# A two-layer graph network with routed experts: the experts' second product as seven block products

## The chip, the cores and the metric

The kernel runs on one core of one Trainium2 chip. A core has five engines with in-order queues of their own: TensorE (PE: matmuls, with the loads of their weights shown apart as PEld), VectorE (DVE), ScalarE (ACT), GpSimd (POOL) and SyncE (SP, which issues most transfers); data lies in SBUF (128 partitions) and products appear in PSUM banks. The metric is the device time of the core in microseconds. A profile is one execution of its own; its time is given beside the median of the runs without a profile.

## The reference

A graph of N = 3327 nodes with D = 256 features goes through two layers. Each adds an aggregation over the dense adjacency matrix `adj`, and then a mixture of eight experts, of which every node uses two:

```
# layer 0
x = x + relu(adj @ (layernorm(x) @ W) + b)
t = layernorm(x)
e1, e2 = top_2(t @ Wg.T + bg);  p1, p2 = softmax of the two scores
x = x + sum over e in (e1, e2):  p_e * (relu(t @ W1[e].T + b1[e]) @ W2[e].T + b2[e])     # hidden 1024
# layer 1
f = tanh(adj * adj), kept where adj > 0 (the 700 largest of a row)
h = tanh(layernorm(x) @ W_proj + b_proj)
x = x + relu(f @ (h @ W_gcn) + b_gcn)
x = x + t + sum over two experts of p_e * (gelu(t @ w1[e] + b1[e]) @ w2[e] + b2[e])      # t = layernorm(x), hidden 256
```

All of it is float32. The change concerns the product with `W2[e]` in layer 0 and the bias and the weight behind it.

## The kernel before

The nodes are padded to 3328, 26 tiles of 128. `x` stays in SBUF; six large buffers of SBUF, the `ring`, hold whatever streams in (pieces of the adjacency matrix, weights of experts, rows), and one more, `pad`, holds the small operands of a block of tokens.

**Layer 0, aggregation** (`aggregate_first`, L482). Thirteen panels of 256 nodes. Pairs of panels are made from seven half-size products in place of eight (`pair`, with sums made by VectorE in place). The last panel is done alone. For each finished pair, `weigh` (L504) multiplies the sums by W and writes to `x`, `route` computes the row norms and the gate scores and picks two experts for each node, and `list_tokens` (L756, through `list_waiting` and `listed`) counts places with two tiny matmuls a tile (L767, L768), turns the scores into weights (the exponential, L759) and scatters each node's normalised row, with its weight (column WT) and its target row (ID), by GpSimd's indirect DMA into a DRAM list sorted by expert (`scatter`, L788). What is left for the last panel, `finish` (L512), is handed to the experts and runs inside their first block. There it first lists the tokens of the last pair (`listed()`), then weighs the last panel's two tiles, then routes that panel.

**Layer 0, experts** (`experts`, L1060). The lists are worked off in blocks of up to SB = 256 tokens of one expert, two groups of 128 each (SG = 2). There are 30 blocks: 26 pair blocks with two groups and 4 with one ("singles"). The first EARLY = 8 blocks are pairs known early; the later order is one single after every four pairs. `step` (L1242) does a block t:

- it issues the loads of block t + 2 on SP's queue (rows xb, W1, b1, W2, b2; each block takes two of the six ring buffers, so three blocks are in flight);
- `first` (L1175): for each of eight chunks of 128 hidden features, two matmuls of 128 weight columns by 256 tokens into a PSUM bank (L1182; two banks, `psh`), then bias and ReLU by ScalarE into `hT` (L1189);
- on block 0 alone, `between` = `finish`;
- `turned` (L1165): TensorE transposes the rows of block t + 1 (L1168), and `copy`, VectorE's tensor_copy in layer 0, brings them to SBUF (L1172);
- `second` (L1192): VectorE makes the target rows (L1202, L1203). For each group eight matmuls with 128 tokens of `hT` as weights and 256 columns of W2 moving are summed in a PSUM bank (L1220; four banks, `psy`); VectorE adds b2 (L1227), multiplies by the token's weight (L1228), and GpSimd scatters the rows into the DRAM array `ys0` (L790).

```
for hc in range(hc_n):
    last_product[:] = [nc.tensor.matmul(ps, lhsT=hT[:, hc, ts(g, P)], rhs=w2[:, hc, :], ...)]
nc.vector.tensor_tensor(y[:, g, :], ps, bb2, ALU.add)
last_y[:] = [nc.vector.tensor_scalar(y[:, g, :], y[:, g, :], xb[:, g, WT : WT + 1], None, ALU.mult)]
```

Matmuls in float32 are two records each in the trace.

**The order on the engines.** Each engine works its queue strictly in order. The order in a queue comes from the framework's scheduler, which works with estimated costs; `tc.issue_after(...)` and the kernel's `behind(...)` (L293) put an instruction behind a given one. `last_y` and `last_product` are the latest instruction of their kinds, for that use.

**Around and after the experts.** After block 1 `load_gate(gates[1])` (L1430) broadcasts the second layer's gate matrix from DRAM to `gate`, an SBUF tile of 128 x 2048, through GpSimd's queue (1 MB); `gate` held the first layer's gate before, for VectorE's products in `scores` (L659). The next use is layer 1's routing. Behind block 27, `add_begun` (L1473) adds outputs of tiles done by then to `x` (six additions, L1304), and behind block 28 `statistics` of 12 tiles (from L337) starts their layernorm. When all 30 blocks are done, `between` (L1521) issues what leads to layer 1: the rest of the outputs is loaded on SP's queue behind the scatters of `ys0`, added, normalised (L371), transposed (L387) and multiplied by the two matrices; the first pieces of the transposed adjacency are loaded and filtered. Then follow layer 1's aggregation (`aggregate`, L430), its experts and the output.

Of the kernel before, what the change touches and what calls it, by code (L numbers as in the profile page):

```python
# [10 lines left out]
F32 = mybir.dt.float32  # L11
# [11 lines left out]
P = 128  # L23
# [104 lines left out]
def gnn_moe_two_layers(  # L128
# [353 lines left out]
    def aggregate_first(b_sb, w, w_sb, begin, count, route, listed, freed):  # L482
# [29 lines left out]
        def finish():  # L512
            if not waiting:
                return
            todo = list(waiting)
            waiting.clear()
            listed()
            for pan, g in todo:
                for it in range(PW // P):
                    weigh(pan, g, it)  # L520
            for _ in route([pan for pan, _ in todo]):
                pass
# [536 lines left out]

    def experts(xlist, ys, group, fixed, n_hidden, func, w1T, b1, w2T, b2, copy, order_of_places, kept=None):  # L1060

# [4 lines left out]
        own_n, all_w2, all_b2, all_b1 = kept or (EARLY + LATE, None, None, None)  # L1066
        several = []
        hc_n = n_hidden // P
# [105 lines left out]

        def first(xT, w1, bb1, n):  # L1175

            hT = blk("narrow" if kept else "wide", hc_n * SB)
            hT = hT.rearrange("p (c b) -> p c b", b=SB)[:, :, 0 : n * P]
            for hc in range(hc_n):
                ps = psh.tile([P, n * P], F32, name="ps_h", tag="ph")  # L1180
                for c in range(DC):
                    nc.tensor.matmul(  # L1182
                        ps,
                        lhsT=w1[:, c, ts(hc, P)],
                        rhs=xT[:, c, :],
                        start=(c == 0),
                        stop=(c == DC - 1),
                    )
                nc.scalar.activation(hT[:, hc, :], ps, func, bias=bb1[:, hc : hc + 1])  # L1189
            return hT  # L1190

        def second(t, late, hT):  # L1192
            _, xb, _, _, w2, bb2 = loaded[t]
            col, n = col_of(t), groups_of(t)
            index = work.tile([P, SG], I32, name="index", bufs=6)[:, 0:n]
            with behind(last_y):
                if t < EARLY:
                    nc.vector.tensor_copy(index, xb[:, :, ID])
                else:
                    _, own, aside = late[0:3]  # L1200
                    index_f = index.bitcast(F32)
                    nc.vector.tensor_tensor(index_f, xb[:, :, ID], own[:, col, 0:n], ALU.mult)  # L1202
                    nc.vector.tensor_tensor(index, index_f, aside[:, col, 0:n], ALU.add)  # L1203
            if t >= own_n:
                e = expert(t, late, [PE, DVE])
# [11 lines left out]
            for g in range(n):  # L1217
# [12 lines left out]
                )]  # L1230
                d = scatter(ys, index[:, g : g + 1], y[:, g, :], "outputs" + group)
                tc.declare_no_dep(d.ins, group="read" + group, reason="not rows read by then")
                outputs.append(d)

# [7 lines left out]
        def step(late, end=always, place=None, between=None):  # L1242
# [7 lines left out]
            _, _, w1, bb1, _, _ = loaded[t]  # L1250
            hT = first(ready.pop(t), w1, bb1, groups_of(t))
            if between:
                between()
            if t + 1 < min(len(loaded), end):
                ready[t + 1] = turned(loaded[t + 1][1], groups_of(t + 1), place)
            second(t, late, hT)

# [118 lines left out]
    def count(pan, k, copied):  # L1376
# [9 lines left out]
        xlist0, ys0, "0", FIXED[0], H, AF.Relu, f0_w1T, f0_b1, f0_w2T, f0_b2,  # L1386
        nc.vector.tensor_copy, BLOCKS0,
    )
# [40 lines left out]

    load_gate(gates[1])  # L1430
    by_feature(None, g1_wp, proj_sb)
# [89 lines left out]
    def between():  # L1521

        normal.clear()
        second.clear()
# [330 lines left out]
```

## Time and profile before

| | us |
|---|---|
| median of 3 runs | 1203.28 (1201.26 to 1204.91) |
| profiled execution, its time | 1216.42 |
| profiled execution, span of the trace | 1214.7 |
| TensorE busy in the span | 1169.4 |
| VectorE, ScalarE, GpSimd busy | 754.7, 524.8, 288.5 |
| layer 0's experts, first to last product | about 298 to 711 |
| mean granted TensorE clock | 0.988 |

Times in the trace count from the start of its span. Busy time is the time in which an engine has an instruction at work; an idle time has beside it, in brackets, the engine and the line of what ended it. An entry such as `x32` in a timeline stands for 32 records in a row without a gap, and its time runs from the first start to the last end, which lies in the pipe behind the last issue; the distance between two starts is the better measure of what a group takes. Three rows of TensorE's timeline, from the stretch in which block 0's `finish` runs:

```profile
308.86 1.97 PE L506 MATMUL ps_o<-proj_sb,xnT 128*128 128x256 f32 x8
310.76 0.66 PE L1168 MATMUL ptb<-ident,ring 128*128 128x128 f32 x4
311.25 1.03 PE L1220 MATMUL ps_y<-ring,pad 128*128 128x256 f32 x4
```

It shows the two tiles of the last panel weighed (four matmuls, eight records), the transposes for block 1, and block 0's second product beginning.

### The profile page before, as it was taken

How to read it: one execution, taken by the hardware profiler on the slowest of the kernel's cores; microseconds unless marked ns; L12 is line 12 of the kernel's file. 1: busy time of each engine (PE TensorE's matmuls, PEld its weight loads, DVE VectorE, ACT ScalarE, POOL GpSimd, SP SyncE). 2: the span in 40 equal slices, each digit the busy share in tenths (PEclk: the TensorE clock that was granted, in tenths of full speed). 3: DMA queues.
4: the chain of work that ended last, by engine and by line, in shares of the span. 5: the costliest groups of instructions: out<-in, count | busy, mean ns of one | idle time of the engine just before them, and what ended most of it. 6: DMA issues, size and time to landing. Idle time of an engine off the chain costs nothing. (4 is left out here: it accounts for less than half of the span.)

```text
span 1214.7 us, 18191 instructions
## 1 busy us (share of the span) xinstructions
PE 1169.4 (96%) x5689; PEld 1001.9 (82%) x5689; DVE 754.7 (62%) x2767; ACT 524.8 (43%) x977; POOL 288.5 (24%) x367
## 2 busy tenths in 40 slices
PE   8999999999899999999999999999999999988973
PEld 7888888888688888888888888888888888877863
DVE  7699999988851111111111469289999998774454
ACT  5689566531122222223222246976546541143321
POOL 1112243143421111111111100022232232264431
PEclk9999999999999999999999999999999999989996
DMA  9895747654465565757565945245445442557686
GB/s 344 177 298 223 247 157 201 234 170 147 152 222 187 184 225 168 237 177 258 185 209 171 382 166 196 76 168 187 160 174 187 168 167 78 173 173 229 207 281 211
DMA packets 123178, 241.59 MB, mean 199 GB/s; under 512 B 24480, under 2 KB 93120, under 8 KB 116160
## 3 DMA queue, kind: packets, MB, share of 16 engines
q1 hardware_dynamic: 108656, 205.59, 51.8%
q0 software_dynamic: 11136, 31.60, 7.1%
q10 hardware_dynamic: 3280, 3.15, 0.8%
q8 instruction: 47, 0.77, 0.3%
q14 instruction: 59, 0.48, 0.1%
HBM read 203.98 MB, written 36.33 MB: 198 GB/s over the span
## 5 line engine op out<-in xcount | busy, mean ns | idle before, releaser
L440 PE MATMUL ps_g<-s,ring 128*128 128x256 f32 x1352 | 294.2, 380 | 0.0
L440 PEld LDWEIGHTS ps_g<-s,ring 128*128 128x128 f32 x1352 | 256.0, 190 | 34.4
L1189 ACT ACTIVATE pad<-ps_h,ring 128x256 f32<-128x256 f32 (+1 forms) x282 | 128.4, 457 | 344.4 <-PE ps_h L1182 311.1
L1182 PE MATMUL ps_h<-pad,ring 128*128 128x256 f32 (+1 forms) x1184 | 255.6, 368 | 6.4 <-ACT pad L1172 3.1
L1182 PEld LDWEIGHTS ps_h<-pad,ring 128*128 128x128 f32 x1184 | 203.5, 191 | 51.6 <-ACT pad L1189 16.0
L1220 PE MATMUL ps_y<-ring,pad 128*128 128x256 f32 x928 | 209.7, 381 | 0.0
L790 POOL DMA_INDIRECT ys<-pad,index x114 | 112.5, 987 | 392.1 <-DVE pad L1228 260.1
L659 DVE SCALAR_TENSOR_TENSOR rt_product<-xn,gate 128x256 f32<-128x256 f32 x400 | 195.3, 488 | 15.4 <-ACT xn L360 2.1
L1220 PEld LDWEIGHTS ps_y<-ring,pad 128*128 128x128 f32 x928 | 173.8, 191 | 22.2 <-issue 0.2
L790 POOL DMA_INDIRECT xlist<-xn,rt_idx x104 | 114.6, 1101 | 151.4 <-DVE ln_nw L347 56.6
L1380 ACT ACTIVATE sign<-ring,below 128x416 bf16<-128x416 f32 x208 | 133.4, 641 | 12.1 <-DMA ring<-in_adjT 6.1
L470 PE MATMUL ps_g<-ring,pad 128*128 128x256 f32 x520 | 115.1, 380 | 1.1 <-DMA ring<-in_adjT 1.1
L1227 DVE TENSOR_TENSOR pad<-ps_y,ring 128x256 f32<-128x256 f32 x64 | 27.1, 424 | 136.6 <-PE ps_y L1220 132.1
L470 PEld LDWEIGHTS ps_g<-ring,pad 128*128 128x128 f32 x520 | 98.4, 190 | 14.6 <-DMA ring<-in_adjT 1.5
L1172 DVE COPY pad<-ptb 128x512 f32<-128x512 f32 (+1 forms) x29 | 18.9, 653 | 144.1 <-PE ptb L1168 144.1
L1545 ACT ACTIVATE ring<-ring 128x3328 f32<-128x3328 f32 x22 | 65.4, 2979 | 87.6 <-DVE ring L1544 50.2
L470 PE MATMUL ps_g<-ring,s 128*128 128x256 f32 x390 | 89.6, 379 | 0.0
L470 PEld LDWEIGHTS ps_g<-ring,s 128*128 128x128 f32 x390 | 74.1, 190 | 10.1
L480 DVE TENSOR_TENSOR ring<-ring,ring 128x768 f32<-128x768 f32 (+1 forms) x80 | 79.7, 1016 | 0.0
L495 PE MATMUL ps_g<-ring,s 128*128 128x256 f32 x312 | 68.7, 380 | 4.3 <-ACT s L360 4.3
L495 PEld LDWEIGHTS ps_g<-ring,s 128*128 128x128 f32 x312 | 59.0, 190 | 13.0 <-ACT s L360 5.2
L1546 ACT ACTIVATE ring<-ring 128x3328 f32<-128x3328 f32 x22 | 65.4, 2978 | 0.6
(221 smaller groups left out, 1108.7 us busy)
## 6 DMA issues: line engine op xcount, KB each, us to landing
ring<-in_adjT SPq DMA_DIRECT2D x50, 1664.0 KB
ring<-in_f_w1T SPq DMA_DIRECT2D x30, 1024.0 KB
ring<-in_f_w2T SPq DMA_DIRECT2D x30, 1024.0 KB
ring<-xlist SPq DMA_DIRECT2D x52, 258.0 KB
ring<-in_f_w SPq DMA_DIRECT2D x36, 256.0 KB
ring<-ys SPq DMA_DIRECT2D x12, 512.0 KB
ring<-in_f_b SPq DMA_DIRECT2D x34, 128.0 KB
xlist<-h2T SPq DMA_DIRECT2D x16, 257.0 KB
```

Of the source, the lines that this page charges most:

```text
L440: nc.tensor.matmul(ps[it], lhsT=chunks[k][:, c, ts(it, P)], rhs=s[:, j, :], start=(j == 0), stop=(j == NT - 1),)
L470: nc.tensor.matmul(ps, lhsT=b[:, c, :], rhs=a[:, c, :], start=(first and c == 0), stop=(c == CJ - 1), skip_group_check=not first,)
L480: nc.vector.tensor_tensor(out[:, part, :], out[:, part, :], other[:, part, :], ALU.add)
L495: nc.tensor.matmul(sums[pan][c], lhsT=s[:, j, ts(c, P)], rhs=piece(pan, j // CJ)[:, j % CJ, :], start=(j == 0), stop=(j == NT - 1),)
L659: nc.vector.scalar_tensor_tensor(product, xn, 1.0, gate[:, e, :], ALU.mult, ALU.mult, accum_out=sc[:, g, e : e + 1],)
L790: d = nc.gpsimd.indirect_dma_start(out=a[:, :], out_offset=bass.IndirectOffsetOnAxis(ap=index, axis=0), in_=rows_, in_offset=None,)
L1182: nc.tensor.matmul(ps, lhsT=w1[:, c, ts(hc, P)], rhs=xT[:, c, :], start=(c == 0), stop=(c == DC - 1),)
L1189: nc.scalar.activation(hT[:, hc, :], ps, func, bias=bb1[:, hc : hc + 1])
L1220: last_product[:] = [nc.tensor.matmul(ps, lhsT=hT[:, hc, ts(g, P)], rhs=w2[:, hc, :], start=(hc == 0), stop=(hc == hc_n - 1),)]
L1380: nc.scalar.activation(sign, piece(pan, k)[:, :, ts(i, GROUP)], AF.Sign, bias=below, accum_out=positive[:, pan, i, k : k + 1],)
L1545: nc.scalar.activation(a, a, AF.Square)
L1546: nc.scalar.activation(a, a, AF.Tanh)
```

## The change

Five edits, all around layer 0's experts.

1. *Seven block products* (`seven=3`: for pair blocks from t = 3 on, 23 of the 26). The second product multiplies a 256 x 1024 matrix of hidden values by a 1024 x 256 matrix. Both are cut into 2 x 2 blocks, and the result is made from seven products of blocks (`second_seven`), each four matmuls of 128 weight columns by 128 columns: 28 matmuls of 128 columns in place of 16 of 256. Ahead of the first product `prepare` makes four sums of halves of W2 on VectorE (128x512 elements each) in the tile `gate`, put behind the previous block's last update (`behind(last_y)`); `difference` makes s3 of hidden halves after the fourth ReLU, and s1, s2, s4 follow the last one (128x512 each). Four PSUM banks hold the results, and two are used twice. Eight `put_in` on VectorE multiply a bank's 128x128 by the tokens' weights and add it to `y`.
2. *Scaled bias* (`weighed_bias`): in those blocks ScalarE writes b2 times the token's weight into `y`, behind the block's own last ReLU, in place of VectorE's addition and scaling.
3. *Copy of the turned rows*: layer 0's `copy` is `nc.scalar.copy` in place of `nc.vector.tensor_copy`, for all blocks.
4. *`finish`*: the last pair's `listed()` comes behind the two `weigh` of the last panel, and all of `between` in a block is put behind the last matmul of that block's first product (`last_product` is now set in `first` as well).
5. *Gate of layer 1*: since `gate` is used for the sums, `load_gate(gates[1])` moves from behind block 1 to the start of `between()`, after the last block.

`place_of` and `put` are the former lines of `second`, now shared.

```diff
--- before.py
+++ after.py
@@ -514,10 +514,13 @@
                 return
             todo = list(waiting)
             waiting.clear()
-            listed()
+            if todo[0][0] < NPAN - 1:
+                listed()
             for pan, g in todo:
                 for it in range(PW // P):
                     weigh(pan, g, it)
+            if todo[0][0] == NPAN - 1:
+                listed()
             for _ in route([pan for pan, _ in todo]):
                 pass

@@ -1057,14 +1060,15 @@
         nc.vector.tensor_tensor(aside, spare_, aside, ALU.subtract)
         return end

-    def experts(xlist, ys, group, fixed, n_hidden, func, w1T, b1, w2T, b2, copy, order_of_places, kept=None):
+    def experts(xlist, ys, group, fixed, n_hidden, func, w1T, b1, w2T, b2, copy, order_of_places, kept=None,
+                seven=None):

         own_n, all_w2, all_b2, all_b1 = kept or (EARLY + LATE, None, None, None)
-        several = []
+        several, last_hidden = [], []
         hc_n = n_hidden // P

         parts = [("w1", DC * n_hidden), ("xb", SG * RW), ("b1", hc_n), ("w2", hc_n * D), ("b2", D)]
@@ -1172,26 +1176,67 @@
             copy(xT, pt)
             return xT

-        def first(xT, w1, bb1, n):
+        def halves(a, k, i):
+            return a[:, k * hc_n // 2 : (k + 1) * hc_n // 2, ts(i, P)]
+
+        def prepare(t):
+
+            w2 = loaded[t][4]
+            flat = gate.rearrange("p e d -> p (e d)")
+            n = hc_n // 2 * P
+            sums = [flat[:, i * n : (i + 1) * n].rearrange("p (c d) -> p c d", d=P) for i in range(4)]
+            t1, t3, t2, t4 = sums
+            b21, b22 = halves(w2, 1, 0), halves(w2, 1, 1)
+            with behind(last_y):
+                nc.vector.tensor_tensor(t1, halves(w2, 0, 1), halves(w2, 0, 0), ALU.subtract)
+                nc.vector.tensor_tensor(t2, b22, t1, ALU.subtract)
+                nc.vector.tensor_tensor(t4, b21, t2, ALU.subtract)
+                nc.vector.tensor_tensor(t3, b22, halves(w2, 0, 1), ALU.subtract)
+            tokens_ = [
+                work.tile([P, DC, 2 * P], F32, name=name, bufs=2).rearrange(
+                    "p c (h d) -> p (c h) d", d=P
+                )
+                for name in ("xnT", "xnT", "h2T", "h2T")
+            ]
+            return sums, tokens_
+
+        def weighed_bias(t):
+
+            xb, bb2 = loaded[t][1], loaded[t][5]
+            y = blk("narrow", SG * D).rearrange("p (g d) -> p g d", d=D)
+            with behind(last_hidden):
+                for g in range(SG):
+                    nc.scalar.activation(y[:, g, :], bb2, AF.Copy, scale=xb[:, g, WT : WT + 1])
+            return y
+
+        def difference(sums, hT):
+
+            a11, a21 = halves(hT, 0, 0), halves(hT, 0, 1)
+            nc.vector.tensor_tensor(sums[1][2], a11, a21, ALU.subtract)
+
+        def first(xT, w1, bb1, n, sums=None):

             hT = blk("narrow" if kept else "wide", hc_n * SB)
             hT = hT.rearrange("p (c b) -> p c b", b=SB)[:, :, 0 : n * P]
             for hc in range(hc_n):
                 ps = psh.tile([P, n * P], F32, name="ps_h", tag="ph")
                 for c in range(DC):
-                    nc.tensor.matmul(
+                    last_product[:] = [nc.tensor.matmul(
                         ps,
                         lhsT=w1[:, c, ts(hc, P)],
                         rhs=xT[:, c, :],
                         start=(c == 0),
                         stop=(c == DC - 1),
-                    )
-                nc.scalar.activation(hT[:, hc, :], ps, func, bias=bb1[:, hc : hc + 1])
+                    )]
+                last_hidden[:] = [
+                    nc.scalar.activation(hT[:, hc, :], ps, func, bias=bb1[:, hc : hc + 1])
+                ]
+                if sums and hc == hc_n // 2 - 1:
+                    difference(sums, hT)
             return hT

-        def second(t, late, hT):
-            _, xb, _, _, w2, bb2 = loaded[t]
-            col, n = col_of(t), groups_of(t)
+        def place_of(t, late):
+            xb, col, n = loaded[t][1], col_of(t), groups_of(t)
             index = work.tile([P, SG], I32, name="index", bufs=6)[:, 0:n]
             with behind(last_y):
                 if t < EARLY:
@@ -1201,6 +1246,62 @@
                     index_f = index.bitcast(F32)
                     nc.vector.tensor_tensor(index_f, xb[:, :, ID], own[:, col, 0:n], ALU.mult)
                     nc.vector.tensor_tensor(index, index_f, aside[:, col, 0:n], ALU.add)
+            return index
+
+        def put(y, index, g):
+            d = scatter(ys, index[:, g : g + 1], y[:, g, :], "outputs" + group)
+            tc.declare_no_dep(d.ins, group="read" + group, reason="not rows read by then")
+            outputs.append(d)
+
+        def second_seven(t, late, hT, sums, y):
+
+            (t1, t3, t2, t4), (s1, s2, s3, s4) = sums
+            _, xb, _, _, w2, _ = loaded[t]
+            index = place_of(t, late)
+            a11, a12, a21, a22 = (halves(hT, k, i) for i in range(2) for k in range(2))
+            b11, b21, b22 = halves(w2, 0, 0), halves(w2, 1, 0), halves(w2, 1, 1)
+            nc.vector.tensor_tensor(s1, a21, a22, ALU.add)
+            nc.vector.tensor_tensor(s2, s1, a11, ALU.subtract)
+            nc.vector.tensor_tensor(s4, a12, s2, ALU.subtract)
+            ps_x, ps_q, ps_b, ps_z = (
+                psy.tile([P, P], F32, name="ps_y", tag="py") for _ in range(4)
+            )
+
+            def multiply(ps, a, b, first=True):
+                for c in range(hc_n // 2):
+                    last_product[:] = [nc.tensor.matmul(
+                        ps, lhsT=a[:, c, :], rhs=b[:, c, :], start=(first and c == 0),
+                        stop=(c == hc_n // 2 - 1), skip_group_check=not first,
+                    )]
+
+            def put_in(g, half_, ps):
+                part = y[:, g, ts(half_, P)]
+                last_y[:] = [nc.vector.scalar_tensor_tensor(
+                    part, ps, xb[:, g, WT : WT + 1], part, ALU.mult, ALU.add
+                )]
+
+            multiply(ps_x, a11, b11)
+            put_in(0, 0, ps_x)
+            multiply(ps_q, a22, t4)
+            put_in(1, 0, ps_q)
+            multiply(ps_b, a12, b21)
+            put_in(0, 0, ps_b)
+            multiply(ps_z, s1, t1)
+            put_in(1, 1, ps_z)
+            multiply(ps_x, s2, t2, False)
+            put_in(0, 1, ps_x)
+            multiply(ps_z, s4, b22, False)
+            put_in(0, 1, ps_z)
+            put(y, index, 0)
+            multiply(ps_x, s3, t3, False)
+            put_in(1, 0, ps_x)
+            put_in(1, 1, ps_x)
+            put(y, index, 1)
+
+        def second(t, late, hT):
+            _, xb, _, _, w2, bb2 = loaded[t]
+            n = groups_of(t)
+            index = place_of(t, late)
             if t >= own_n:
                 e = expert(t, late, [PE, DVE])
                 w2 = all_w2[:, ds(e, 1), :, :].rearrange("p o c d -> p (o c) d")
@@ -1228,9 +1329,7 @@
                 last_y[:] = [nc.vector.tensor_scalar(
                     y[:, g, :], y[:, g, :], xb[:, g, WT : WT + 1], None, ALU.mult
                 )]
-                d = scatter(ys, index[:, g : g + 1], y[:, g, :], "outputs" + group)
-                tc.declare_no_dep(d.ins, group="read" + group, reason="not rows read by then")
-                outputs.append(d)
+                put(y, index, g)

         ready = {}

@@ -1248,12 +1347,19 @@
             if t not in ready:
                 ready[t] = turned(loaded[t][1], groups_of(t))
             _, _, w1, bb1, _, _ = loaded[t]
-            hT = first(ready.pop(t), w1, bb1, groups_of(t))
+            sums = prepare(t) if seven and t >= seven and groups_of(t) == SG else None
+            hT = first(ready.pop(t), w1, bb1, groups_of(t), sums)
+            if sums:
+                y = weighed_bias(t)
             if between:
-                between()
+                with behind(last_product):
+                    between()
             if t + 1 < min(len(loaded), end):
                 ready[t + 1] = turned(loaded[t + 1][1], groups_of(t + 1), place)
-            second(t, late, hT)
+            if sums:
+                second_seven(t, late, hT, sums, y)
+            else:
+                second(t, late, hT)

         def steps_to(late, stop):
             while len(started) < stop:
@@ -1384,7 +1490,7 @@

     layer0 = experts(
         xlist0, ys0, "0", FIXED[0], H, AF.Relu, f0_w1T, f0_b1, f0_w2T, f0_b2,
-        nc.vector.tensor_copy, BLOCKS0,
+        nc.scalar.copy, BLOCKS0, seven=3,
     )

     def tiles_of(pans):
@@ -1427,7 +1533,6 @@
         list_waiting()

-    load_gate(gates[1])
     by_feature(None, g1_wp, proj_sb)
     nc.gpsimd.dma_start(out=gnn_b_sb, in_=g1_bg[0:1, :].partition_broadcast(P))
     ng = NPAN * PW // GROUP
@@ -1520,6 +1625,7 @@

     def between():

+        load_gate(gates[1])
         normal.clear()
         second.clear()
         waiting = []
```

## The prediction

> **What bounds the kernel now.** I read the busy shares first, then the engines' busy time by stages, then TensorE's timeline inside the stage that the change touches, and last VectorE's timeline where that stage ends. The chain that ended last covers only the final 13 us of the span (output rows coming back, the last additions) and says nothing of this change.
>
> ```profile
> PE 1169.4 (96%) x5689; PEld 1001.9 (82%) x5689; DVE 754.7 (62%) x2767; ACT 524.8 (43%) x977; POOL 288.5 (24%) x367
> ```
>
> ```profile
> 305.70:310.80 5.10, 2.55 (x17) 1.87 (x16) 4.46 (x23) 0.57 (x2) 0.32 (x2) 1.00 0.00 0
> ...
> 337.00:683.00 346.00, 345.69 (x1695) 291.25 (x1695) 72.47 (x259) 95.04 (x208) 50.29 (x52) 1.00 0.64 209
> 683.00:711.40 28.40, 28.40 (x135) 23.75 (x134) 19.64 (x61) 7.57 (x16) 4.60 (x4) 1.00 0.57 220
> 711.40:763.00 51.60, 50.87 (x258) 42.71 (x257) 40.99 (x112) 33.39 (x71) 1.35 (x3) 1.00 0.55 207
> ```
>
> The columns of the second fence are the stretch, its length, then PE, PEld, DVE, ACT, POOL busy, PE's clock, DMA share. The first layer's experts run from about 298 to 711: TensorE is busy 345.69 of 346 us there, VectorE only 72.5, ScalarE 95. So a microsecond taken from TensorE in that stretch is a microsecond of the kernel, so long as VectorE keeps up. After 711.4 TensorE still fills 50.87 of 51.60, so the gain isn't met by another wait at once. One block, then two widths of matmul side by side:
>
> ```profile
> 612.46 1.05 PE L1182 MATMUL ps_h<-pad,ring 128*128 128x128 f32 x8
> 613.36 0.60 PE L1220 MATMUL ps_y<-ring,pad 128*128 128x256 f32 x2
> 613.79 1.05 PE L1182 MATMUL ps_h<-pad,ring 128*128 128x128 f32 x8
> ...
> 618.15 7.16 PE L1182 MATMUL ps_h<-pad,ring 128*128 128x256 f32 x32
> 625.15 0.60 PE L1168 MATMUL ptb<-ident,ring 128*128 128x128 f32 x4
> 625.59 7.07 PE L1220 MATMUL ps_y<-ring,pad 128*128 128x256 f32 x32
> 632.49 0.81 PE L1182 MATMUL ps_h<-pad,ring 128*128 128x256 f32 x3
> ```
>
> A pair block lasts 632.49 - 618.15 = 14.34 us: first product, four transposes of the next block, second product. Each program matmul is two records. From start to start, 32 records of 256 columns take 632.49 - 625.59 = 6.90 us, 0.216 each; 8 records of 128 columns (blocks of one group) take 613.36 - 612.46 = 0.90, 0.112 each. I use these starts, not the means of the groups, which are latencies with the pipe's end in them.
>
> [...]
>
> ```profile
> L1304 DVE TENSOR_TENSOR x<-x,ring 128x512 f32<-128x512 f32 x24 | 16.1, 690 | 14.0 <-DMA ring<-ys 11.8 <-issue 2.1
> L693 DVE TENSOR_TENSOR rt_gt<-rt_gt,rt_eq 128x128 f32<-128x128 f32 x16 | 4.7, 292 | 0.5
> ```
>
> **The change part by part.** *Seven products.* Of 26 pair blocks those from t = 3 on, 23, lose 16 matmuls of 256 columns (6.90 us) and get 28 of 128: 28 x 2 x 0.112 = 6.26 us. Gain 0.645 us a block, 14.8 for 23. No trace shows 128-column matmuls for 6 us on end; the bounds are 0.112 (gain 0.645) and the groups' mean busy share per record, 24.8 us/176 = 0.141 (a loss of 1.0). I take 0.112, since the two rows shown have the same form, operands in SBUF and a new weight each.
>
> *Their preparation on VectorE.* Each block gains four sums of w2 halves, three more sums s1, s2, s4 and one s3 of hidden halves (128x512 each, 8 x 0.69 = 5.5 us) and eight PSUM updates of 128x128 (0.29 each, 2.3), and loses two additions (0.42), two scalings (0.35) and the 0.69 copy of x. VectorE's load is about 8.1 us in a 13.7 us block: it fits, so what counts is the order. Let T be the end of the block's first product. The four transposes end at T + 0.44; the products, 0.894 us each, start at 0.44 (x), 1.33 (q), 2.23 (b), 3.12 (z), 4.02 (s2), 4.91 (s4) and 5.81 (s3). The last ReLU is done at T + 0.67, as the trace has it, so s1 is there at 1.4, s2 at 2.1, s4 at 3.1, each before it is multiplied. x's bank must be emptied before the s2 product at 4.02: done by 2.4. z's must be before 4.91: its update follows z's end at 4.02, done at 4.5. The second use of x ends at 4.91, is emptied at 5.4, needed at 5.81. The least spare is 0.4 us. The sums for the next block follow the last update (T + 7.3) and end at T + 10.3; they are wanted at T + 13.7 + 1.3. No stall in a steady block. If the spare fails by 0.2 us in each of 21 blocks it costs 4 us; below nothing isn't possible here, as TensorE has no idle time to give back. w2 of the next block, for which VectorE now waits, was issued two blocks earlier.
>
> *Scaled bias and copy on ScalarE.* Two scaled copies of 128x256 (0.59 at most, from such an activation in SBUF) and the copy of x, 0.585 instead of 0.69: ScalarE gets some 1.8 us, 5.5 of 13.7. The bias stands behind the block's ReLUs, at T + 1.9, before the first update at 2.1 needs it; the copy follows at T + 2.5, wanted at T + 6.7. Cost nothing, hidden under the second product. If the cover were gone, the first update would move by at most 0.6.
>
> *The last two blocks.* Here VectorE has other work, and the new sums queue behind it:
>
> ```profile
> 684.09 5.76 DVE L1304 TENSOR_TENSOR x<-x,s 128x1024 f32<-128x1024 f32 x5
> ...
> 689.88 1.22 DVE L1304 TENSOR_TENSOR x<-x,s 128x1024 f32<-128x1024 f32 x1
> ...
> 698.42 0.75 DVE L337 BATCH_NORM_STATS2 ln_st<-x 128x6 f32<-128x256 f32 x2
> ```
>
> In before's times: at t = 28 the first sum comes after five of the six additions (689.8) and the fourth at about 693.4, while product q wants it at 691.5. The order of the built kernel fills part of this with eight records of the next block's first product; that one ends at 704.7 instead of an ideal 703.8: 0.9 lost. At t = 29 twelve row statistics (4.7 us) run from the end of block 28's updates, about 699.4, to 704.1; then the four sums, s3 and small operations between them, 5 x 0.69 + 0.7 + 0.2, so t4 is ready about 708.5. Product q wants it at 705.6: TensorE stands 2.9 us, and 0.5 once more before s4. Together 0.9 + 2.9 + 0.5 + 0.2 (the last product's small wait) = 4.5 lost. Bounds: nothing lost, or 6.5, since a TensorE idle for so long may run at half clock afterwards: records took 0.45 us, not 0.216, in the row below after some 3 us of gaps, but not after 2.43 at 305.7. [...]the trace shows it for gaps that sum to 3.07. I take no half clock.
>
> ```profile
> 1077.79 3.62 PE L1220 MATMUL ps_y<-ring,pad 128*128 128x256 f32 x8
> ```
>
> *Last pair's listing.* Before, TensorE waits until 308.12 for the listing's counts, then counts, then weighs two tiles (1.9 us) from 308.86. Now the weighing is put first and could fill the wait. But its second tile needs a PSUM bank that the eighth ReLU frees, and on ScalarE that ReLU stays queued behind an exponential that waits for VectorE (TensorE's timeline, then ScalarE's):
>
> ```profile
> 308.12 0.17 PE L767 MATMUL pr<-rt_both,before 128*128 128x8 bf16 x1 [2.43 <-DVE rt_both L697]
> ```
>
> ```profile
> 308.94 0.21 ACT L759 ACTIVATE rt_d<-rt_d 128x4 f32<-128x4 f32 x1 [3.60 <-DVE rt_d L724]
> 309.05 0.46 ACT L1189 ACTIVATE pad<-ps_h,ring 128x256 f32<-128x256 f32 x1
> ```
>
> The exponential runs at 308.94, the ReLU ends at 309.51, the second tile is weighed 309.6 to 310.46, the counts end at 311.2, and the transposes start there instead of 310.76: +0.44. Bounds: -2.4 (all of the wait filled) to +0.7. The last pair's rows are scattered some 2 us later on POOL and are wanted blocks later.
>
> *The gate load.* It moves from after block 1 to behind the first layer's last product, in POOL's queue ahead of the last group's scatter. About 1 us of POOL and 1 MB (about 3 us of that queue) delay that scatter and the output loads behind it: from 4.2 to about 5.7 us after TensorE's last product. Those outputs reach TensorE through VectorE's normalised rows, ready 3.3 us before their transposes at 731.9 in before: hidden, with some 1.8 to spare. If that cover were gone it would cost at most 1.5. gate's first use is near 791.
>
> *Sum.* 21 x 0.645 = 13.5 gained; the last two blocks 4.5 - 1.3 = 3.2 lost; listing 0.44 lost: -9.9. The profiled execution took 1216.42 (span 1214.7) and would take 1206.5. It is 13.1 above the median of the runs shown, 1203.28, on which I set the same difference: 1193.4, call it 1193.5.
>
> **The rivals.** *All 23 blocks keep their gain*: the queues let the sums in early, or the listing fills its wait. Then -14.8 + 0 = 1188.5; against it, the built order has the statistics first. *The tail costs more*: half clock (+2), a late output load (+1.5), 0.1 us of stall in 21 blocks (+2): 1199. For it: gaps of 3 us did it once; against: 2.97 at 319.9 did not. *Slower*: the weight loads don't hide. [...]if every record in a long run waits for its weights, 0.141 each is 28 x 2 x 0.141 = 7.9 us, +1.0 x 23 = +23, and with the last blocks and the listing +28: 1231. It decides from 0.123 us a record (6.90/56); 0.112 at two places speaks against. *No change*: stalls of 0.45 us in every steady block, if VectorE's updates are 0.8 us later than I reckon; within 0.3% of 1203.3.
>
> **How the numbers follow.** Forecast (my sum, 1191 to 1197) 0.55; all gains kept 0.17; tail costs more 0.15; no change 0.07; slower 0.06. The range 1187.5 to 1200.5 holds the first three, leaving 0.13 out. About 0.3% (3.6 us) can be told from no change here: faster 0.86, same 0.08, slower 0.06.
>
> **What would show it.** Right: a pair block of 13.7 us; seven products in 6.26; TensorE's stretch from 352 to 683 as full as before; a gap of 2.5 to 3.5 us at t = 29 that names VectorE and gate; the first block's transposes 0.2 to 0.6 us later. Wrong: 128-column records further apart than 0.112, small gaps at the third to seventh product, a half clock near 709, or, later on, TensorE waiting for output loads near 730.

## The result, and the profile after

| | before | after |
|---|---|---|
| median of 14 runs each | 1204.82 us (1200.76 to 1207.07) | 1195.24 us (1188.30 to 1200.76) |
| ratio after/before, 95% interval | | 0.9925 (0.9905 to 0.9946) |
| profiled execution, its time and span | 1216.42, 1214.7 | 1194.71, 1192.9 |
| the kernel before, profiled once more | 1204.69, 1202.9 | |

The change makes the kernel 0.75% faster, 9 to 10 us. The two first profiles differ by 21.7 us, which is more than the change is worth. A second profile of the kernel before (experiment 5) lies at its median, and the table below compares with that one. All times in it are from the start of one TensorE record to the start of another.

| stretch of TensorE's work | before, again | after | difference | in the prediction's sum |
|---|---|---|---|---|
| block 0's first product to block 1's transposes | 13.10 | 12.63 | -0.5 | +0.4 |
| from there to the end of block 29 | 397.34 | 386.07 | -11.3 | -10.3 |
| from there to layer 1's aggregation | 51.54 | 52.95 | +1.4 | 0 |
| layer 1's aggregation | 294.93 | 294.93 | 0 | 0 |
| layer 1's experts to the last product | 127.32 | 127.71 | +0.4 | 0 |

The sum is -10.0, as predicted within 0.1, but partly because errors cancel. In both executions TensorE ran at half rate for a while in block 0 (0.427 us for a record of 256 columns instead of 0.216, see experiment 2); in the changed kernel 0.45 us of that loss lies in the second row, in the one before all of it in the first. Up to block 1's first product both take 20.45 us, so the first row is worth nothing and the blocks after it -11.75. First the page's busy shares: TensorE lost work, and VectorE gained 116 us against the first profile.

```profile
PE 1152.2 (97%) x6241; PEld 1005.0 (84%) x6241; DVE 871.1 (73%) x3013; ACT 557.6 (47%) x1053; POOL 295.4 (25%) x367
```

One pair block on TensorE's timeline after the change:

```profile
605.92 7.16 PE L1224 MATMUL ps_h<-pad,ring 128*128 128x256 f32 x32
612.91 0.60 PE L1172 MATMUL ptb<-ident,ring 128*128 128x128 f32 x4
613.35 1.06 PE L1272 MATMUL ps_y<-ring,pad 128*128 128x128 f32 x8
614.24 1.06 PE L1272 MATMUL ps_y<-gate,pad 128*128 128x128 f32 x8
615.14 1.06 PE L1272 MATMUL ps_y<-ring,pad 128*128 128x128 f32 x8
616.03 1.95 PE L1272 MATMUL ps_y<-gate,xnT 128*128 128x128 f32 x16
617.82 1.06 PE L1272 MATMUL ps_y<-ring,h2T 128*128 128x128 f32 x8
618.71 1.06 PE L1272 MATMUL ps_y<-gate,h2T 128*128 128x128 f32 x8
```

The seven products run from 613.35 to 619.60 (605.92 + the block's 13.68): 6.25 us for 56 records, 0.1117 each, without a gap. The tiles after the arrow tell which product it is: ring and pad for halves of W2 and of the hidden values, gate for sums of W2, xnT and h2T for sums of hidden values. As the diff has it, the fifth and seventh product are added to what the first one's bank holds and the sixth to the fourth's, so one bank takes three products and one takes two. The group's mean of one is 275 ns, more than twice its true pace.

The windows over that block and over the last two pair blocks (columns as in the prediction):

```profile
605.92:619.60 13.68, 13.68 (x93) 12.18 (x92) 7.98 (x18) 5.06 (x11) 1.17 (x1) 1.00 0.77 254
668.30:698.79 30.49, 27.43 (x181) 24.31 (x180) 27.93 (x81) 9.65 (x21) 3.64 (x3) 1.00 0.57 217
```

In the block TensorE is full and VectorE has 7.98 of 13.68 us. In the last two blocks (t = 28 and 29) VectorE has more than TensorE: 27.93 of 30.49. There the gap stands that was forecast for t = 29, and it names the fourth sum:

```profile
693.33 1.16 PE L1272 MATMUL ps_y<-gate,pad 128*128 128x128 f32 x8 [2.50 <-DVE gate L1193]
```

### The profile page after: what moved, and what is told of

Same layout as the page of the kernel before. It is cut to its first block, busy times and chain, and to the rows that moved or that the text cites. A ratio compares the mean times of both kernels' runs of the same rounds, so it can differ in the third digit from the quotient of the medians.

```text
span 1192.9 us, 19772 instructions
## 1 busy us (share of the span) xinstructions
PE 1152.2 (97%) x6241; PEld 1005.0 (84%) x6241; DVE 871.1 (73%) x3013; ACT 557.6 (47%) x1053; POOL 295.4 (25%) x367
## 5 line engine op out<-in xcount | busy, mean ns | idle before, releaser
L1224 PEld LDWEIGHTS ps_h<-pad,ring 128*128 128x128 f32 x1184 | 201.1, 191 | 47.3 <-ACT pad L1232 11.5
L793 POOL DMA_INDIRECT ys<-pad,index x114 | 117.0, 1027 | 366.5 <-DVE pad L1279 250.4
L1279 DVE SCALAR_TENSOR_TENSOR pad<-ps_y,ring,pad 128x128 f32<-128x128 f32 x184 | 61.9, 348 | 47.9 <-PE ps_y L1272 47.7
L1263 DVE TENSOR_TENSOR xnT<-pad 128x512 f32<-128x512 f32 x23 | 15.9, 691 | 59.5 <-ACT pad L1232 59.5
L776 POOL COPY xn<-rt_w 128x4 f32<-128x4 f32 x26 | 4.9, 199 | 211.1 <-DVE rt_w L738 211.1
L1321 PE MATMUL ps_y<-s,pad 128*128 128x256 f32 (+1 forms) x200 | 49.6, 388 | 0.1
```

Source lines behind the costliest of these rows:

```text
L793: d = nc.gpsimd.indirect_dma_start(out=a[:, :], out_offset=bass.IndirectOffsetOnAxis(ap=index, axis=0), in_=rows_, in_offset=None,)
L1224: last_product[:] = [nc.tensor.matmul(ps, lhsT=w1[:, c, ts(hc, P)], rhs=xT[:, c, :], start=(c == 0), stop=(c == DC - 1),)]
```

## The experiments

Experiments 1 to 4 and 5 to 8 were timed on two chips where the kernel before takes 1204.2 and 1204.6 us, 9 to 11 on a third, where it takes 1218.0; so for those only ratios are compared. All ratios are to the kernel before; the changed kernel's is 0.9925 (0.9905 to 0.9946).

**1. No seven products.** `seven=None` takes out the seven products with their sums and the scaled bias (edits 1 and 2); edits 3 to 5 stay.

```diff
-        nc.scalar.copy, BLOCKS0, seven=3,
+        nc.scalar.copy, BLOCKS0, seven=None,
```

> The second product by 16 matmuls of 256 columns in every block; the copy on ScalarE, the last pair's listing behind the weighing and the late gate load are kept. My theory (the seven products carry all of the gain, the other edits cost a little): 0.5 us slower than the kernel before at the first block and up to 0.8 at the gate load, so +0 to +1.5 us, 1204 to 1206.5 where before is 1204.8; pair blocks 14.34 us apart. Rival (a good part of the gain is the 3 us stall in block 1 that the changed kernel's trace no longer shows, and comes with the other edits): 3 to 4 us faster than before.

Ratio 1.0005 (0.9994 to 1.0017): 1205.06 us, within the theory's range. Blocks 1 to 29 took 398.27 us (397.34 in the kernel before). So edits 3 to 5 are worth nothing measurable here, and the whole gain comes with the seven products. Two things this run does not show: the scaled bias alone wasn't tried, and the gate's late load has no price here. With `gate` free, the load was issued 47 us ahead of the last product; experiment 4 prices it.

**2. The last pair listed first again.**

```diff
-            if todo[0][0] < NPAN - 1:
-                listed()
+            listed()
...
-                with behind(last_product):
-                    between()
+                between()
```

> The changed kernel with the last pair listed ahead of the weighing again, and block 0's tail of the aggregation no longer put behind the first product. My theory: from the first record of block 0's first product to the transposes of block 1 12.1 us as before, not 12.6; within noise of the changed kernel (-0.5 us). Rival (the listing order is what removed the 3 us stall in block 1): the stall is back and the kernel is 2.5 us slower than the changed one, 1197.5.

Ratio 0.9910 (0.9894 to 0.9925), 1194.03 us: no difference from the changed kernel, and no stall in block 1, so the rival fell. But the stretch took 13.07 us, not 12.1. The reason is in what follows the wait. Here are the same two tiles of the last panel weighed in the kernel before, profiled again:

```profile
309.36 0.17 PE L767 MATMUL pr<-rt_both,before 128*128 128x8 bf16 x1 [2.08 <-DVE rt_both L697]
...
310.09 3.38 PE L506 MATMUL ps_o<-proj_sb,xnT 128*128 128x256 f32 x8
```

The same eight records took 1.97 us in the first profile. Behind a gap TensorE at times runs at half rate, 0.427 us a record (the last section has what the traces show of it). The old order took 12.14 us at full rate and 13.1 with half rate (two executions), the new one 11.65 to 11.78 at full rate (experiments 1, 3, 4, 6) and 12.63 in the changed kernel, with half rate that goes on behind the border.

The 0.4 us between the full rates isn't the order's. In the first profile VectorE came to the listing later: the first count runs 9.50 us behind block 0's first record there, but 9.15 in the kernel before again and 9.03 in this experiment (310.32 behind 301.29). With 9.03 to 9.15, the counts' 0.74 and the weighing's 1.90 at full rate, the old order would take an estimated 11.7 to 11.8 us, as long as the new one. And with half rate block 1's first product starts 20.42 us behind block 0's here, 20.45 in the changed kernel. The order is worth nothing.

**3. Plain products in the last two blocks.**

```diff
-            sums = prepare(t) if seven and t >= seven and groups_of(t) == SG else None
+            sums = prepare(t) if seven and seven <= t < 28 and groups_of(t) == SG else None
```

> Seven products in blocks 3 to 27 only; the last two pair blocks by 16 matmuls. My theory (VectorE is the bound of the last two blocks, since the sums queue behind additions and statistics): the 2.5 us gap is gone, from block 28's first record to the end of block 29 28.3 us as before and not 30.5, so 2.2 us faster than the changed kernel, 1193. Rival (the gap only takes the place of later waits, for rows that VectorE normalises or for output loads): TensorE waits as much at the next transposes, and the time is that of the changed kernel, 1195.

Ratio 0.9881 (0.9859 to 0.9903), 1188.79 us: three times the gain expected, and just below the changed kernel's interval. The last two blocks took 28.24 us and not 30.49, so 2.25 less, as the theory has it:

```profile
666.31:694.55 28.24, 28.24 (x134) 23.63 (x133) 19.03 (x60) 8.12 (x17) 4.60 (x4) 1.00 0.72 277
```

With `gate` free after block 26, the scheduler also issues its load early, 31 us ahead of the last product, and the next stage took 51.53 us in place of 52.95. The rest of the 7.7 us between the two profiles is the half rate that this execution didn't show in block 0 (1.3) and 2.6 us in layer 1's experts, where the kernels vary from one execution to the next.

**4. The gate's load behind the last scatter.**

```diff
-        load_gate(gates[1])
+        with behind(outputs[-1:]):
+            load_gate(gates[1])
```

> The changed kernel with the gate's load put behind the last scatter of the block outputs in GpSimd's queue. My theory (the 1 MB ahead of the last scatter delays the first output load from 4.2 to 8.4 us behind TensorE's last product, and so the 0.77 us gap before the normalised rows of tile 12): the output load is issued some 4.2 us behind the last product, the gap is gone, 0.8 us faster. Rival (the load delays them from behind as well, or VectorE's late updates do it): the output load still comes 7 us or more behind, the gap stays.

Ratio 0.9895 (0.9873 to 0.9916), 1191.10 us; this interval overlaps with the changed kernel's, so the traces decide. GpSimd's queue in the changed kernel, then SyncE's queue, then VectorE and TensorE:

```profile
700.46 0.58 POOL L320 DMA_DIRECT2D gate<-gate  x1
701.35 1.04 POOL L793 DMA_INDIRECT ys<-pad,index  x1 [0.30 <-issue]
```

```profile
707.17 0.93 SPq L1396 DMA_DIRECT2D ring<-ys  x2
```

```profile
712.90 2.48 DVE L1410 TENSOR_TENSOR x<-x,ring 128x1024 f32<-128x1024 f32 x2 [7.89 <-DMA ring<-ys]
```

```profile
720.22 0.67 PE L387 MATMUL pt<-ident,xn 128*128 128x128 f32 x4 [0.77 <-DVE xn L371]
```

And GpSimd's and SyncE's queue with the load moved:

```profile
696.75 0.96 POOL L793 DMA_INDIRECT ys<-pad,index  x1 [0.30 <-DMA ys<-pad,index]
697.71 0.58 POOL L320 DMA_DIRECT2D gate<-gate  x1
```

```profile
699.56 0.93 SPq L1396 DMA_DIRECT2D ring<-ys  x2
```

The first load of outputs is issued 8.4 us behind the end of TensorE's last product (698.79) in the changed kernel, 4.8 (694.79) with the edit; the gap is gone and the stage takes 51.53 us. Of the 3.6 us between them, 0.6 are a later start of the last scatter (2.55 us behind the last product, 1.95 with the edit), and 3.0 come between that scatter and the load. The load's price isn't constant: 1.4 us in the changed kernel's profile, 4.6 in experiment 2's, where a gap of 2.67 us was followed by half rate, and 0.4, 0.6 and 1.2 in experiments 9, 6 and 7.

**5. The kernel before, again.** No edit.

> The kernel before, unchanged, profiled once more, to see which of its stalls are its own. My theory: the 2.97 us stall in block 1 and the long last stage (137.6 us from the end of layer 1's aggregation to the last product, where five other profiled executions took 124.4 to 128.6) were accidents of one execution: here the stall is gone, the last stage takes 124 to 129, the span is about 1203. Rival: they belong to the kernel and come again, span near 1214.

1204.69 us, span 1202.9: the stall in block 1 was gone and the last stage took 127.3 us. So neither belongs to every execution of the kernel. The three profiles from the third chip (experiments 9 to 11), however, show both again: stalls of 1.7 and 1.0 us or the like in block 1, and a last stage of 135.3 to 139.2. The first profile of the kernel before has the marks of that chip or of one like it; that it was taken there is argued, not shown.

**6. The sums ahead of VectorE's other work.** `make(t)` runs `prepare(t)` and keeps its result for `step`.

```diff
+        layer0.make(28)
         with behind(last_y):
             add_begun()
         layer0.step(late)
+        layer0.make(29)
         with behind(last_y):
             statistics(0, BEGUN, begun_stats)
```

> The changed kernel with the four sums of block 28 ahead of the six additions and those of block 29 ahead of the twelve statistics in VectorE's queue. Theory A (the order in the queue makes the 2.5 us gap, as the prediction had it): the gap is gone and 2.5 us are gained, 1192.7. Theory B (VectorE is full from block 27's end to the first transposes of the next stage, so whatever is put first the rest comes late): the gap of 2.5 us goes, but TensorE waits nearly as long for statistics and normalised rows; -0.5 us.

Ratio 0.9908 (0.9885 to 0.9932), 1193.25 us: no difference from the changed kernel. On its timeline the 2.50 us gap is replaced:

```profile
679.04 2.09 PE L1272 MATMUL ps_y<-gate,xnT 128*128 128x128 f32 x16 [0.58 <-DVE xnT L1263]
...
692.86 2.24 PE L1272 MATMUL ps_y<-gate,xnT 128*128 128x128 f32 x16 [1.60 <-DVE xnT L1263]
695.63 1.16 PE L1272 MATMUL ps_y<-ring,h2T 128*128 128x128 f32 x8 [0.53 <-DVE pad L1279]
```

These three waits sum to 2.7 us, where the changed kernel has 0.56 and 2.50, and the two blocks take 30.67 us against 30.49. VectorE is busy for 27.88 of them. Theory B's time holds: VectorE is nearly full there, and this order only chose which product waits. But the waits are for sums of hidden values (L1263) and an update (L1279), not for statistics and normalised rows as theory B said. One other order was tried; that no order does better isn't shown.

**7. The exponential behind the eighth ReLU.**

```diff
-            nc.scalar.activation(w, w, AF.Exp)
+            with behind(layer0.last_hidden if len(layer0.started) == 1 else ()):
+                nc.scalar.activation(w, w, AF.Exp)
```

> The changed kernel with the listing's exponential put behind block 0's eighth ReLU on ScalarE. My theory (the 2.6 us gap in the weighing is that ReLU queued behind an exponential that waits for VectorE): the gap shrinks to the 0.3 to 0.6 us by which the listing's selection on VectorE comes later than the second tile, and block 0's first record to block 1's transposes takes 9.5 to 10 us instead of 11.7 to 12.6; 2 to 2.5 us faster than the changed kernel, 1193. Rival (the tiny count matmuls wait for VectorE to the same moment anyway): the gap moves to them in full, no gain.

Ratio 0.9911 (0.9885 to 0.9936), 1193.97 us, not to be told from the changed kernel. First the changed kernel, then the edited one:

```profile
310.60 2.07 PE L506 MATMUL ps_o<-proj_sb,xnT 128*128 128x256 f32 x4 [2.57 <-ACT pad L1232]
```

```profile
306.96 1.89 PE L506 MATMUL ps_o<-proj_sb,xnT 128*128 128x256 f32 x8
...
311.06 0.66 PE L1173 MATMUL ptb<-ident,ring 128*128 128x128 f32 x4 [1.00 <-DVE gnn_t L403]
```

The gap of 2.57 us is gone, so it was that ReLU; but the transposes then wait 1.00 us for VectorE to empty the bank of the weighing, behind its selection. The stretch takes 11.01 us, 0.7 less than the changed order at full rate, not 2. Half right. In this execution the 2.50 us gap at t = 29 was followed by half rate, which cost another 1.6 us.

**8. Three mendings together**: the edits of 3 and 7, and `load_gate(gates[1])` after block 27 in place of `between`.

> Three mendings of the changed kernel together: the exponential behind the eighth ReLU, the last two pair blocks with 16 matmuls, and the gate's load behind block 26's products, when its tile comes free, so that it lies ahead of no late scatter. My theory adds up what the single runs gave against the changed kernel (-2.3, -2.4 to -2.7 and -1.4 to -4.6; the plain tail and the gate overlap, since either keeps the next stage at 51.5 us): -7 to -8 us, about 1187. Rival (the gains overlap in full): 1188.8, as with the plain tail alone.

Ratio 0.9877 (0.9852 to 0.9902), 1188.56 us. The rival's number: with the plain tail the gate's load is early anyway, and the exponential's 0.7 us is under what can be told. By their ratios this and experiment 3 are the fastest versions, 15 to 16 us below the kernel before, and the only two whose intervals lie clear of the changed kernel's.

**9. The copy on VectorE again.**

```diff
-        nc.scalar.copy, BLOCKS0, seven=3,
+        nc.vector.tensor_copy, BLOCKS0, seven=3,
```

> The changed kernel with the copy of the turned rows on VectorE again; it sits between s1 and s2 in VectorE's queue. This tests the spare of 0.4 us that my reckoning gives a steady block. My theory: 0.6 us more ahead of s2 eat the spare, z's bank is emptied at T + 5.1 instead of 4.5 where the s4 product wants it at 4.91, so each of some 20 blocks stands 0.2 to 0.3 us and lasts 13.9 to 14.0 us instead of 13.68: 4 to 6 us slower than the changed kernel, about 1200. Rival (the spare is larger, or the copy hides elsewhere): 13.68 as before, no difference.

Ratio 0.9921 (0.9898 to 0.9943): no difference from the changed kernel, and steady blocks of 13.68 us. My expectation fell. VectorE's timeline in one block of this kernel:

```profile
617.84 0.69 DVE L1263 TENSOR_TENSOR xnT<-pad 128x512 f32<-128x512 f32 x1 [2.82 <-ACT pad L1232]
618.45 0.69 DVE L1176 COPY pad<-ptb 128x512 f32<-128x512 f32 x1
619.05 0.68 DVE L1264 TENSOR_TENSOR xnT<-xnT,pad 128x512 f32<-128x512 f32 x1
...
621.29 0.35 DVE L1279 SCALAR_TENSOR_TENSOR pad<-ps_y,ring,pad 128x128 f32<-128x128 f32 x1 [0.17 <-PE ps_y L1272]
```

The copy delays the chain by 0.60 us, but ahead of z's update VectorE had waited 0.54 us for TensorE in the changed kernel and still waits 0.17 here. The spare of 0.4 us that I had worked out counts from z's end on TensorE. VectorE can't start that update sooner, and had been waiting for it, so work ahead of it uses up this wait first and leaves the 0.4 us alone. And VectorE's operations start 0.60 us apart, not 0.69: their ends overlap.

**10. Late gate and exponential, 23 blocks with seven products.** The edits of 4 and 7.

> The changed kernel with the gate's load behind the last scatter and the exponential behind the eighth ReLU, all 23 blocks with seven products. Against the version with the plain tail (1188.6) it should show the price of seven products in the last two blocks alone. My theory: 2.7 us, 1191; blocks 1 to 29 take 385.6 to 387 us instead of 383.4. Rival (with the late gate mended the tail costs nothing): 1188.5.

Ratio 0.9904 (0.9887 to 0.9921), against 0.9877 for the version with the plain tail; the intervals overlap, so the times don't show the 3 us between them, which would agree with the 2.25 us of the traces. The 2.5 us gap at t = 29 is there as ever, and the last two blocks take 30.5 us. Blocks 1 to 29 took 390.47 us, outside the 385.6 to 387 expected, since on this chip blocks 1 and 2 have waits that the others don't show.

**11. The mended version, seven products from block 1.**

```diff
-        nc.scalar.copy, BLOCKS0, seven=3,
+        nc.scalar.copy, BLOCKS0, seven=1,
```

> The three mendings and seven products from block 1 on instead of block 3, so in 23 blocks again. My theory: VectorE is half full with routing and planning in blocks 1 and 2, but the sums come through: twice 0.66 us, 1.3 us faster than the mended version, 1187.3; at worst the stalls there eat it, 1188.6. Rival (as in the last two blocks VectorE becomes the bound, behind the routing and the planning of the lists): 2 to 3 us slower than it, 1191.

Ratio 0.9887 (0.9857 to 0.9918): inconclusive. Blocks 1 and 2 ran their seven products without a gap, but block 4 stood 0.56 us for its turned rows, and block 0's second product, which has no part in the edit, ran at half rate for eight records. Nothing is gained that could be told.

## Why the prediction was right, point by point

**Steady blocks: right, 0.66 us each instead of 0.645.** A block takes 13.68 us in place of 14.34. Experiment 3 has 21 such blocks and plain ones at the end: 397.34 - 383.36 = 14.0 us against the kernel before, profiled again. The pace of 0.112 us for 128 columns, read off eight records in a block of one group, held over 56 (0.1117), and the rival of weight loads that don't hide (0.141) is out. No steady block has a gap on TensorE. The spare was worked out with durations where starts count, and this error didn't matter (experiment 9).

**The last two blocks: right in kind, 2.25 us lost net instead of 3.2.** They took 30.49 us, and 28.24 with plain products. The gap at t = 29 was 2.50 us and not 2.9, with none before s4, since VectorE's operations follow at 0.60 us and not 0.69. At t = 28 TensorE stood 0.56 us, for ScalarE's copy of the turned rows, where 0.9 from VectorE was forecast. The prediction took no half clock behind the gap. That held in the changed kernel's profile and not in experiment 7's, so it was partly luck. The reason was put too narrowly: the prediction blamed the order of VectorE's queue. In experiment 6 another order gave the same end, and VectorE's load, 27.9 us in some 30.5, fits both.

**The listing: too dear, 0 instead of +0.44.** The step "the exponential runs at 308.94" failed as a term of the sum: it was taken from the first profile, 10.32 us behind block 0's first record, and it ran 9.85 to 9.99 behind it in the kernel before again, in the changed kernel and in experiments 1 to 4 and 6, with either order (10.46 in experiment 9, on the third chip). And the eight tiny matmuls took 0.26 us (312.47 to 312.73), not 0.74, since the cumulative sums that they had waited for one by one were ready. The chain itself (exponential, ReLU, bank, second tile) was right, as experiment 7 shows. That block 1's transposes came 12.63 us behind block 0's first record, where the prediction's times give 12.58, is luck: the half rate is in it.

**The gate load: wrong, +1.4 in this profile instead of 0.** The step "from 4.2 to about 5.7 us ... hidden, with some 1.8 to spare" failed. The later start of the last scatter was right (2.55 us behind the last product instead of 1.59; 0.6 of the 0.96 is the gate's, the rest the later end of the block itself). But the prediction itself put the transfer at about 3 us and then counted 0.5 of it; behind the scatter the load came 3.2 us later than before. Together that is 4.2 us, more than the 3.3 us of slack. What comes out varies from 0.4 to 4.6 us, with half rate in the dearest case.

**The sum was right in part by luck.** The two large terms were near: -14.0 for -13.5 and +2.3 for +3.2. With the listing's 0 for +0.44 the changed kernel would have gained 1.9 us more than forecast. The gate's +1.4 and 0.4 us of chance in layer 1's experts took that back. The profile's own offset of 13.1 us from the median, which the prediction carried over unchanged, wasn't there in the second profile of before.

## What to carry to other kernels

Read the pace of matmuls and of VectorE's operations from start to start (here 0.112 and 0.60 us); the means of their groups (0.275 and 0.69) hold the pipe's end as well. Profile the old kernel twice before reading a small term off one place in one trace. When work moves from the bound engine to one with room, look for the few places where that engine is full already, and leave the old form there: here the last 2 of 23 blocks gave back 2.25 us, and leaving them plain also freed a buffer early enough to load it unseen. A transfer put into a queue ahead of another can delay it by more than its issue: here by 0.6 us of issue and 3 us behind it.

## What the runs showed of the hardware

TensorE's half rate (0.427 us for a record of 256 columns and 0.213 for one of 128, where 0.216 and 0.112 are usual) looks like chance: the gap of 2.50 us at t = 29 was followed by it in experiment 7, and not in the changed kernel. The record of the granted clock in the traces shows more. In the first profile of the kernel before the clock fell to 0.50 at 1075.52, 1099.41, 1184.75 and 1198.40 us, in the changed kernel's at 310.25, 1163.58 and 1177.23. The last phase of each lies behind the last product, to the end of the trace; the others lasted 3.41 us, the one at 1075.52 twice that. Within one execution all starts are a whole number of 3.41 us apart: 7, 25 and 4 times in the first of these profiles, 250 and 4 times in the second, and 222, 7, 18 and 7 times in experiment 9 (310.74, 1068.50, 1092.39, 1153.84 and 1177.73 us). So in each of these executions the starts lie on a grid of 3.41 us, and not on the same one: 310.25 and 1075.52 are 224.2 times 3.41 us apart. Two steps of that length in experiment 7, then the one of the changed kernel that holds most of the same gap (columns as above):

```profile
689.14:692.55 3.41, 1.31 (x11) 1.31 (x12) 3.41 (x13) 0.07 (x1) 0.00 (x0) 1.00 0.00 0
692.55:695.97 3.42, 3.42 (x18) 3.42 (x17) 2.30 (x12) 0.00 (x0) 0.00 (x0) 0.50 0.00 0
```

```profile
689.06:692.47 3.41, 1.77 (x13) 1.48 (x11) 3.41 (x13) 1.74 (x4) 0.00 (x0) 1.00 0.00 1
```

In experiment 7 nearly the whole gap lies in one step, with TensorE busy for 1.31 of 3.41 us, and the next one ran at a clock of 0.50. In the changed kernel the gap is split over two, with 1.77 us busy in the one shown, and the clock stayed at 1.00.

How much idle time in a step goes with it is my estimate, with each record counted at its pace from start to start. In the first profile of the kernel before and in the changed kernel's, from 20 us on, the seven steps at full clock with 2.18 to 3.06 us idle were followed by half clock, and none of those with 2.02 or less. In the stretch from 290 to 730 us of all thirteen executions the eight with 2.15 us or more were followed by it, and none with 1.99 or less. Elsewhere in the traces three steps with an estimated 2.1 to 2.3 us weren't followed by it, so these figures are no sharp border. The idle time need not be one gap: a tiny matmul at 1075.13 us parts it in the first profile (waits of 1.66 and 0.27 us), and in experiment 11 the gap shortly ahead of the slow records (at 312.72) was 1.00 us. A phase cost 1.3 us in block 0 of the changed kernel, 1.6 in experiment 7 and 1.7 in experiment 11.

Chips differ: the kernel before took 1204 us on two and 1218 us on a third, and the traces of the third show waits in block 1 (1.72 us in experiment 9, 1.71 and 1.03 in experiment 11) and layer 1 experts of 135.3 to 139.2 us (127.3 in the kernel before again), which those of the first two don't. What causes them wasn't tried.
